# Layer 0 and layer 2 hand-over in a four-layer graph kernel: the last group's large row operations on GpSimd, layer 0's two halves together, the last two output transfers from SyncE

## Chip, cores and metric

One Trainium2 chip, one core of it. The metric is the device time of one execution in microseconds (us): three runs of the kernel before took 1114.72, 1115.99 and 1119.29 us, median 1115.99. Inside the core, TensorE (PE in the profile) does matrix products, VectorE (DVE) and ScalarE (ACT) do elementwise work, GpSimd (POOL) does elementwise work on data in SBUF only, and SyncE (SP) issues transfers. Each engine runs its own list of instructions in order.

## The reference

Four layers over 4096 nodes with 64 features and a dense 4096 x 4096 matrix `adj` of zeros and ones. Each layer is `x = layernorm(x + f(x, adj))`:

- layer 0: `h = (adj @ x + x) / deg`, then `relu([x, h] @ W + b)`, divided by its row norm
- layers 1 and 3: hyperbolic attention. For each pair i, j with an edge, a sigmoid of `left[i] + right[j]` weights the logarithmic map of x[j] at x[i]; the sums over j go through the exponential map and a projection
- layer 2: row i sums `x[j] @ weight` over its last 100 neighbours, with weights that halve from one neighbour to the next

```python
def _layernorm(x, axis=-1, eps=1e-5):
    m = jnp.mean(x, axis=axis, keepdims=True)
    v = jnp.var(x, axis=axis, keepdims=True)
    return (x - m) / jnp.sqrt(v + eps)
...
support_t = jnp.einsum('ij,ijd->id', adj_att, x_local)
return proj(expmap(x, support_t, c), c)
...
x = _layernorm(x + _L0_gnn_ref(x, adj, L0_gnn_W, L0_gnn_b), axis=-1)
```

## The kernel before

Nodes lie in four groups (`GROUPS` = 3, 2, 1, 0) of 1024, each of eight blocks (`WB`) of 128 partitions. One tile of a group's rows, `grp(...)`, is 128 x 512 floats (eight blocks of 64 features); one number for each row, `nums(...)`, is 128 x 8. Every layer walks over the four groups of target nodes and, inside each, over the 32 source blocks j from last to first, two blocks (one `g`) to a 1 MB load of `adj` from the SyncE queue into one of six buffers (`load`).

Two kinds of work share the engines. The pair work fills most of the time. In attention (`attend`, L1025) one block j needs six matrix products into `z` (L1059, L1062, L1065), a sigmoid and a square on ScalarE (L1074, L1077), one VectorE operation (L1080), and once for each g a VectorE operation over 128 x 2048 (L1082) and eight products that add up (L1037). Call the two VectorE operations T (L1080, 128 x 1024, reads PSUM and SBUF) and S (L1082, 128 x 2048, reads SBUF twice). The row work turns a finished group's sums into the next layer's tables. It is written as Python generators that `later(...)` puts into two queues; after each block of pairs `tick` lets each queue emit its next few instructions, and what a generator yields says after how many ticks it goes on. PE and ACT keep the order in which instructions were emitted in layers 0 and 2 (`manual_schedule`), a planner places the rest.

For one group that ends layer 0 (`end_0`, L1357) the row work is: for each half of the group, eight pairs of products into a PSUM tile (L1365, L1366), a reciprocal and two VectorE operations (L1369, L1371, L1373); then relu, a square on GpSimd (L1378), a row sum, an inverse root, two 128 x 512 operations (L1384, L1385); then `norm_rows` and `prepare`. `end_2` does the same after layer 2, with its own beginning (L1488, L1492, L1498).

- `norm_rows` (L862): mean, difference, square on GpSimd (L869), row sum (L872), inverse root of ten small operations, and L877, which writes the next layer's `x`.
- `prepare` (L882) and its inner `second`: small operations give `ym` (L895); L896 makes `y` from `x` and `ym`; ScalarE casts `y` three times (L899 to L901) into `ys` and `yd`; GpSimd fills ten extra columns from `hl` (L907 to L912); L915 writes the rest of `ys` (the part of `y` that the cast lost); L921 makes `w` from `x` and `g`; L923 makes `xe` from `w` and `m`, the operand of L1037. PE then turns `ys` and `yd` block by block (L943, 32 products) through PSUM, ScalarE copies each of the four results into `hi_lo`, `lo_hi`, `src` and `dst` (L947), eight products give L955, L965 reads them, and `left` and `right` follow (L975 to L977), after a logarithm on ScalarE (L950, L951).

The last group, 0, ends a layer, so its row work lies beside the first pairs of the next attention layer. `attend` calls `need((layer, 2 * g // WB))`, so the pairs of blocks 7 to 0, the last quarter of a pass, stand behind group 0's tables.

`spare` (a list) holds a second PSUM tile for row work in layers 0 and 2; `take` goes back and forth between the two tiles, and `held` counts those in use. `spare_ends` after layer 0 runs ticks until none is held.

At the end of an attention layer `move` (L1098) does the row work of a group's sums: on GpSimd for groups 3, 2 and 1, on VectorE for group 0. After layer 3 `store` (L1611) sends a group of `out` from the ScalarE queue (L1612).

Of the kernel before, what the change touches and what calls it, by code (L numbers as in the profile page):

```python
# [10 lines left out]
F32 = mybir.dt.float32  # L11
# [8 lines left out]
P = 128  # L20
N = 4096
D = 64
# [3 lines left out]
SB = W // P  # L26
# [5 lines left out]
WB = WW // P  # L32
# [26 lines left out]
def gnn_stack_kernel(  # L59
# [15 lines left out]
    nc = tc.nc  # L75
    V = nc.vector
# [492 lines left out]
    def stream(fits):  # L569

        with ExitStack() as st:
# [10 lines left out]
            GROUPS = tuple(reversed(range(NW)))  # L582
# [8 lines left out]
            queues, place, done, held = ([], []), [0, 0], set(), []  # L591
# [54 lines left out]
            def soon():  # L646


                return 0 if place[0] in (0, 2) else 1
# [7 lines left out]
            def near():  # L657

                return 3 if place[0] == 0 else 1
# [21 lines left out]
            def free():  # L681
                while held:
                    yield 1
# [18 lines left out]
            def grp(name, bufs=None):  # L702
                kw = {"bufs": bufs} if bufs else {}
                return row.tile([P, WB, D], F32, name=name, **kw)

            def nums(name, n=WB):
                return row.tile([P, n], F32, name=name)

            def over(v):
                return v[:, :, None].to_broadcast([P, v.shape[1], D])  # L710

            def rsqrt(a, name):

# [60 lines left out]
            xe = keep.tile([P, NB, D], F32, name="xe")  # L774
# [23 lines left out]
            ys = keep.tile([P, WB, 3 * D + 10], F16, name="ys")  # L798
# [43 lines left out]
            def curved(c, name, least):  # L842
# [16 lines left out]
                V.tensor_scalar(short, root, least, None, ALU.mult)  # L859
                return c, c2, sc, rsc, of_y, root, short, by_root, by_short  # L860

            def norm_rows(layer, s, v, x2_to):  # L862

                m, v2, sq = nums("n_m"), nums("n_v2"), grp("sq")
                V.tensor_reduce(m, v, AX.X, ALU.add)
                V.tensor_scalar(m, m, 1.0 / D, None, ALU.mult)
                yield soon()
                V.tensor_sub(v, v, over(m))  # L868
                nc.gpsimd.tensor_mul(sq, v, v)  # L869
                yield soon()  # L870
                yield soon()
                V.tensor_reduce(v2, sq, AX.X, ALU.add)  # L872
                yield soon()
                V.tensor_scalar(m, v2, 1.0 / D, 1e-5, ALU.mult, ALU.add)
                r = rsqrt(m, "n_r")
                yield soon()
                V.tensor_mul(x_of(layer)[:, blocks(s), :], v, over(r))  # L877
                V.tensor_mul(x2_to, r, r)
                V.tensor_mul(x2_to, x2_to, v2)
                yield soon()  # L880

            def prepare(layer, s, att, b_att, curve, least, good, small):  # L882
# [3 lines left out]
                at, cols = blocks(s), slice(s * WW, (s + 1) * WW)  # L886
                xg, bg, rbg = x_of(layer)[:, at, :], b[:, at], rb[:, at]
# [5 lines left out]

                ym, y = nums("ym"), grp("y")
                V.tensor_scalar(ym, rbg, sc, None, ALU.mult)  # L895
                V.tensor_mul(y, xg, over(ym))  # L896

                def second():
                    nc.scalar.copy(ys[:, :, :D], y)  # L899
# [11 lines left out]
                    for k, of in ((7, 0), (8, 0), (9, 1)):  # L911
                        nc.gpsimd.tensor_scalar(  # L912
                            ed[:, :, k], hl[:, :, of], -2.0 / UNIT, None, ALU.mult
                        )
                    V.tensor_sub(ys[:, :, D : 2 * D], y, ys[:, :, :D])  # L915

                    m, g, w = nums("m"), nums("g"), grp("xw")
                    V.tensor_scalar(g, cx2[:, at], 1.0, 1.0 / D, ALU.add, ALU.mult)
                    V.tensor_scalar(m, rbg, CUBE / UNIT, None, ALU.mult)
                    yield 1  # L920
                    V.tensor_add(w, xg, over(g))  # L921
                    yield 1
                    V.tensor_mul(xe[:, at, :], w, over(m))  # L923

                    q, q1, t = nums("q"), nums("q1"), nums("tt")
                    V.tensor_scalar(q, x2[:, at], least, c, ALU.max, ALU.mult)
# [27 lines left out]
                    for k in range(WB):  # L954
                        nc.tensor.matmul(  # L955
                            p[:, k, :], hi_lo[:, s * WW + k * P : s * WW + (k + 1) * P], att,
                            start=True, stop=True,
# [32 lines left out]
                    yield 1  # L990

                later(second(), True, after(small))
                yield 1

# [252 lines left out]
            def supports(s):  # L1247
# [40 lines left out]
                out=enter, in_=pass_by, compare_op=ALU.is_gt, fill=0.0, base=0,  # L1288
# [14 lines left out]
            with ExitStack() as lp:  # L1303
# [10 lines left out]
                xw = own.tile([P, NB, D], F32, name="xw")  # L1314
                sum_w = own.tile([P, D + 1], F32, name="sum_w")
                count_w = own.tile([D + 1, D + 1], F32, name="count_w")
# [39 lines left out]

                def end_0(s, tops):  # L1357
                    z = grp("z0")
                    for h, (top, low) in enumerate(tops):
                        yield from free()  # L1360
                        t = take(F32, P, SB, P)
                        for k in range(SB):
                            cols = slice(k * P, (k + 1) * P)
                            to = t[:, k, : D + 1]
                            nc.tensor.matmul(to, top[:, cols], sum_w, start=True, stop=False)  # L1365
                            nc.tensor.matmul(to, low[:, cols], count_w, start=False, stop=True)  # L1366
                        at = slice(s * WB + h * SB, s * WB + (h + 1) * SB)
                        d = nums("deg", SB)
                        V.reciprocal(d, t[:, :, D])  # L1369
                        zz = z[:, h * SB : (h + 1) * SB, :]  # L1370
                        V.tensor_mul(zz, t[:, :, :D], over(d))  # L1371
                        held.pop()
                        V.tensor_add(zz, zz, xw[:, at, :])  # L1373
                        if h == 0:
                            yield near()
                    V.tensor_scalar(z, z, 0.0, None, ALU.max)
                    sq, n2 = grp("sq"), nums("n2")
                    nc.gpsimd.tensor_mul(sq, z, z)  # L1378
                    yield 1
                    V.tensor_reduce(n2, sq, AX.X, ALU.add)  # L1380
                    V.tensor_scalar(n2, n2, 1e-24, None, ALU.max)
                    n = rsqrt(n2, "n")
                    yield 1
                    V.tensor_mul(z, z, over(n))  # L1384
                    V.tensor_add(z, z, x0[:, blocks(s), :])  # L1385
                    yield 1
                    yield from norm_rows(1, s, z, x2[:, blocks(s)])
                    yield from prepare(
                        1, s, att1, batt1_sb, curve1, 1e-15, good[:, 0], 70
                    )  # L1390

                with tc.manual_schedule(engines=FIXED):
                    for s in GROUPS:
# [3 lines left out]
                        for g in reversed(range(NB // 2)):  # L1397
# [5 lines left out]
                            for k in (1, 0):  # L1403
                                j = 2 * g + k
                                for lhs, accs, m in parts:
                                    for h in range(2):
                                        at = k * WW + h * W
                                        nc.tensor.matmul(  # L1408
                                            accs[h][:m], lhs[:, j, :], edge[:, at : at + W],
                                            start=j == BLOCKS[0], stop=j == BLOCKS[-1],  # L1410
                                        )
                            if g == s * WB // 2 + 1:

                                for lhs, accs, m in parts:
                                    for h in range(2):
                                        for k in range(SB):
# [3 lines left out]
                                                start=False, stop=False,  # L1420
# [9 lines left out]
                        tops = []  # L1430
                        for h in range(2):
                            top = sb.tile([P, W], F32, name="top")
                            nc.scalar.copy(top, sums[h])
                            low = sb.tile([D + 1, W], F32, name="low")
                            nc.scalar.copy(low, counts[h][: D + 1])
                            tops.append((top, low))
                        later(end_0(s, tops))
                        if s > 0:
                            own_of = linear(0, s - 1, w0_sb[:D, :], own_part)
# [169 lines left out]
            place[0] = 3  # L1609

            def store(s):  # L1611
                nc.scalar.dma_start(out[:, blocks(s), :], x_of(4)[:, blocks(s), :])  # L1612
                yield 1

            attention(3, curve3, (4, 1, 1, 1), store)


            V.tensor_reduce(fits, odd, AX.X, ALU.add)
            V.tensor_scalar(fits, fits, 0.0, None, ALU.is_equal)
            t, g = nums("m1", 1), nums("g1", 1)  # L1620
# [80 lines left out]
```

## Time and profile before

| what | us |
|---|---|
| median of three runs | 1115.99 |
| the profiled execution | 1117.97 |
| its span | 1116.2 |
| PE busy (share of the span) | 996.4 (89%) |
| DVE busy | 912.1 (82%) |
| ACT busy | 803.4 (72%) |
| POOL busy | 271.0 (24%) |
| layer 0, its loads | 0 to about 183 |
| first pairs of layer 1 on DVE | 201.8 |
| first pairs of layer 3 on DVE | 763.5 |
| last S of layer 3 | 1077.2 |

The page of the profile gives busy time for each engine, then the span in 40 slices, the transfers, the chain of waits that ended last, and groups of instructions. The timeline lists single instructions: start in us, duration in us, engine, line, operation, what it writes and reads, and in square brackets the idle time of the engine before it and what ended that. A busy share of 82% for DVE is an average: it is near full in the attention layers and low in layers 0 and 2 and in the last 40 us.

### The profile page before, as it was taken

The numbers are of one execution on the slowest core, as the hardware profiler recorded it, in microseconds if no ns is written. First come the engines' busy times: TensorE is split into PE (matmuls) and PEld (weight loads), VectorE is DVE, ScalarE is ACT, GpSimd is POOL, SyncE is SP. The second block draws the span as 40 slices with busy tenths as digits, with TensorE's granted clock in tenths as the row PEclk, the third lists the DMA queues.
The fourth block names the chain that finished last, engine by engine and source line by source line (L and its number), as shares of the span: only waits on it lengthen the run. The fifth ranks groups of instructions, "written<-read, shape, count | busy, mean of one in ns | idle before, by whom it ended". The sixth has DMA issues, their size and how long they took to land.

```text
span 1116.2 us, 13744 instructions
## 1 busy us (share of the span) xinstructions
PE 996.4 (89%) x4861; PEld 393.9 (35%) x4949; DVE 912.1 (82%) x1452; ACT 803.4 (72%) x892; POOL 271.0 (24%) x649
## 2 busy tenths in 40 slices
PE   4998889789999999998998997788899999999960
PEld 2455455233333333332333332223333333333320
DVE  5677977999999999999366476447989999999965
ACT  0013122989999999896776788889899999998940
POOL 0011210010144443424500010000001544345281
PEclk8899999899999999999999999899899999999995
DMA  8899999546576576663987986587456766666300
GB/s 339 346 422 376 366 423 382 204 136 243 195 238 219 184 244 217 218 210 130 360 306 275 370 277 228 203 276 252 166 194 221 247 215 216 238 224 224 126 1 23
DMA packets 38581, 271.63 MB, mean 243 GB/s; under 512 B 4710, under 2 KB 4710, under 8 KB 5734
## 3 DMA queue, kind: packets, MB, share of 16 engines
q1 hardware_dynamic: 37440, 269.50, 66.4%
q10 hardware_dynamic: 1062, 1.15, 0.3%
q8 instruction: 41, 0.67, 0.2%
q14 instruction: 38, 0.31, 0.1%
HBM read 269.58 MB, written 1.05 MB: 242 GB/s over the span
## 4 chain that ended last, share of the span: by engine, by line
PE 58%; DVE 22%; ACT 9%; POOL 4%; DMA 4%; issue 3%; ACTq 0%; SPq 0%; POOLq 0%; DVEq 0%
PE acc L1037 14%; PE z L1563 9%; DVE t L1082 8%; DVE t L1080 6%; PE z L1062 6%; PE acc L1408 6%; PE z L1059 6%; PE z L1065 6%; PE acc L1575 3%; DMA edges<-in_adj_dram 3%; ACT sq L1077 3%; ACT sq L1570 3%; ACT sig L1074 2%; PE z L1575 1%; PE aux L943 1%
## 5 line engine op out<-in xcount | busy, mean ns | idle before, releaser
L1080 DVE SCALAR_TENSOR_TENSOR t<-z,sig 128x1024 f32<-128x1024 f32 x256 | 308.9, 1218 | 13.8 <-ACT sq L1077 7.7
L1077 ACT ACTIVATE sq<-z,turn 128x1024 f32<-128x1024 f32 x256 | 278.1, 1112 | 46.2 <-PE z L1065 17.8
L1082 DVE SCALAR_TENSOR_TENSOR t<-sq,t 128x2048 f32<-128x2048 f32 x128 | 297.4, 2323 | 0.5
L1074 ACT ACTIVATE sig<-left_b,right 128x1024 f32<-128x1024 f32 x256 | 286.2, 1147 | 1.8 <-DVE t L1080 1.3
L1037 PE MATMUL acc<-t,xe 128*64 128x512 f32 x1024 | 255.6, 611 | 18.4 <-DVE t L1082 17.9
L1062 PE MATMUL z<-lo_hi,hi_lo 128*128 128x512 f16 x512 | 194.6, 380 | 3.8 <-issue 1.0
L1065 PE MATMUL z<-dst,src 74*128 74x512 f16 x512 | 195.6, 382 | 0.0
L1059 PE MATMUL z<-edges,two_i 128*128 128x512 bf16 x462 | 181.5, 393 | 8.1 <-DVE t L1080 8.1
L1570 ACT ACTIVATE sq<-z,at_edge 128x512 bf16<-128x512 f32 (+1 forms) x192 | 149.4, 829 | 44.4 <-PE z L1563 41.3
L838 DVE SCALAR_TENSOR_TENSOR t<-edges 128x2048 bf16<-128x2048 f32 x32 | 73.0, 2288 | 52.8 <-DMA edges<-in_adj_dram 52.8
L1037 PEld LDWEIGHTS acc<-t,xe 128*64 128x64 f32 x1024 | 63.8, 137 | 147.5 <-issue 83.6
L1563 PE MATMUL z<-edges,pass_by 128*128 128x512 bf16 x241 | 87.6, 400 | 18.4 <-ACT sq L1570 17.6
L1059 PEld LDWEIGHTS <-two_i 128*128 128x128 bf16 x512 | 50.2, 98 | 127.5 <-issue 82.8
L1408 PE MATMUL acc<-edges,first 128*128 128x512 bf16 x241 | 78.0, 400 | 16.1 <-DMA edges<-in_adj_dram 15.5
L1563 PE MATMUL z<-edges,enter 128*128 128x512 bf16 x240 | 85.0, 397 | 0.5
L1408 PE MATMUL acc<-edges,third 128*65 128x512 bf16 x256 | 81.4, 400 | 0.9 <-issue 0.4
L838 DVE SCALAR_TENSOR_TENSOR junk<-edges 128x2048 bf16<-128x2048 f32 x32 | 73.1, 2286 | 4.6 <-DMA edges<-in_adj_dram 4.3
L1065 PEld LDWEIGHTS <-src 74*128 74x128 f16 x512 | 49.3, 96 | 70.5 <-issue 8.4
L1062 PEld LDWEIGHTS <-hi_lo 128*128 128x128 f16 x512 | 50.4, 98 | 58.0 <-issue 12.5
L1575 PE MATMUL acc<-sq,halves 128*64 128x512 bf16 x384 | 61.6, 398 | 2.6 <-issue 1.6
L869 POOL TENSOR_TENSOR sq<-z 128x512 f32<-128x512 f32 x8 | 14.1, 1759 | 162.2 <-DVE z L868 139.5
L1133 POOL TENSOR_TENSOR w_att<-x,u 128x512 f32<-128x512 f32 x6 | 15.6, 2599 | 142.9 <-ACT u L1128 142.9
(375 smaller groups left out, 939.4 us busy)
## 6 DMA issues: line engine op xcount, KB each, us to landing
edges<-in_adj_dram SPq DMA_DIRECT2D x256, 1024.0 KB, 5.0
x<-in_x_dram SPq DMA_DIRECT2D x4, 256.0 KB
out_dram<-x ACTq DMA_DIRECT2D x4, 256.0 KB
w_sb<-in_L_gnn_W_dram ACTq DMA_DIRECT2D x1, 32.0 KB, 5.9
w_twice<-in_L_gnn_weight_dram ACTq DMA_DIRECT2D x2, 16.0 KB, 8.2
given<-in_L_gnn_b_dram ACTq DMA_DIRECT2D x1, 0.2 KB
given<-in_L_gnn_bias_dram ACTq DMA_DIRECT2D x1, 0.2 KB
given<-in_L_gnn_b_att_dram ACTq DMA_DIRECT2D x1, 0.0 KB
```

The lines of the kernel that those rows point to most:

```text
L838: V.scalar_tensor_tensor(junk, a, 0.0, a, ALU.not_equal, ALU.not_equal, accum_out=odd[:, n : n + 1])
L1037: it = nc.tensor.matmul(acc[h * D : (h + 1) * D, :], xe[:, j, :], t[:, k, h * W : (h + 1) * W], start=j == BLOCKS[0], stop=j == BLOCKS[-1],)
L1059: nc.tensor.matmul(half, two_i, edge[:, at : at + W], start=True, stop=False)
L1062: nc.tensor.matmul(half, hi_lo[:, of], lo_hi[:, to], start=False, stop=False)
L1065: last = nc.tensor.matmul(half, src[:, of], dst[:, to], start=False, stop=True)
L1074: nc.scalar.activation(sig, left_b, AF.Sigmoid, bias=right[:, j : j + 1])
L1077: nc.scalar.activation(sq[:, k], zp, AF.Square, bias=turn, scale=-1.0 / UNIT)
L1080: V.scalar_tensor_tensor(t[:, k], zp, 0.0, sig, ALU.max, ALU.mult)
L1082: V.scalar_tensor_tensor(t, sq, HIGH**2, t, ALU.add, ALU.mult)
L1408: nc.tensor.matmul(accs[h][:m], lhs[:, j, :], edge[:, at : at + W], start=j == BLOCKS[0], stop=j == BLOCKS[-1],)
L1563: nc.tensor.matmul(z[:, h : h + W], lhs, rhs[:, h : h + W], start=j == BLOCKS[0], stop=True, skip_group_check=True,)
L1570: nc.scalar.activation(w, z[:, :n], AF.Exp, bias=at_edge, scale=-LN2)
```

## The change

A helper `large_on(s)` picks GpSimd for group 0 and VectorE for the others, and five 128 x 512 operations go through it: L877, L896, L915, L921, L923. It acts after layer 0 and after layer 2, so on ten instructions in all. In `end_0` both halves take their PSUM tiles and issue their products one after the other where `spare` is there, and VectorE's part for both follows with no yield between. The transfers of groups 1 and 0 to `out` go to the SyncE queue.

```diff
+            def large_on(s):
+                return nc.gpsimd if s == GROUPS[-1] else V
...
-                V.tensor_mul(x_of(layer)[:, blocks(s), :], v, over(r))
+                large_on(s).tensor_mul(x_of(layer)[:, blocks(s), :], v, over(r))
...
-                V.tensor_mul(y, xg, over(ym))
+                large_on(s).tensor_mul(y, xg, over(ym))
...
-                    V.tensor_sub(ys[:, :, D : 2 * D], y, ys[:, :, :D])
+                    large_on(s).tensor_sub(ys[:, :, D : 2 * D], y, ys[:, :, :D])
...
-                    V.tensor_add(w, xg, over(g))
+                    large_on(s).tensor_add(w, xg, over(g))
                     yield 1
-                    V.tensor_mul(xe[:, at, :], w, over(m))
+                    large_on(s).tensor_mul(xe[:, at, :], w, over(m))
...
-                    for h, (top, low) in enumerate(tops):
-                        yield from free()
-                        t = take(F32, P, SB, P)
...
-                        held.pop()
-                        V.tensor_add(zz, zz, xw[:, at, :])
-                        if h == 0:
+                    yield from free()
+                    for some in ((0, 1),) if spare else ((0,), (1,)):
+                        ts = []
+                        for h in some:
+                            top, low = tops[h]
+                            t = take(F32, P, SB, P)
...
+                            ts.append((h, t))
+                        for h, t in ts:
...
+                            V.tensor_mul(zz, t[:, :, :D], over(d))
+                            V.tensor_add(zz, zz, xw[:, at, :])
+                        if some == (0,):
                             yield near()
+                    held.clear()
...
-                nc.scalar.dma_start(out[:, blocks(s), :], x_of(4)[:, blocks(s), :])
+                queue = nc.sync if s <= 1 else nc.scalar
+                queue.dma_start(out[:, blocks(s), :], x_of(4)[:, blocks(s), :])
```

More of the change, by code (lines that the diff above doesn't have):

```diff
@@ L1358, in end_0 @@
                     z = grp("z0")
-                    for h, (top, low) in enumerate(tops):
-                        yield from free()
-                        t = take(F32, P, SB, P)
[L1362 to L1371, printed above, removed]
-                        held.pop()
-                        V.tensor_add(zz, zz, xw[:, at, :])
-                        if h == 0:
+                    yield from free()
[4 more added lines that the diff above has]
+                            t = take(F32, P, SB, P)
+                            for k in range(SB):
+                                cols = slice(k * P, (k + 1) * P)
+                                to = t[:, k, : D + 1]
+                                nc.tensor.matmul(to, top[:, cols], sum_w, start=True, stop=False)
+                                nc.tensor.matmul(to, low[:, cols], count_w, start=False, stop=True)
+                            ts.append((h, t))
+                        for h, t in ts:
+                            at = slice(s * WB + h * SB, s * WB + (h + 1) * SB)
+                            d = nums("deg", SB)
+                            V.reciprocal(d, t[:, :, D])
+                            zz = z[:, h * SB : (h + 1) * SB, :]
+                            V.tensor_mul(zz, t[:, :, :D], over(d))
+                            V.tensor_add(zz, zz, xw[:, at, :])
+                        if some == (0,):
                             yield near()
+                    held.clear()
                     V.tensor_scalar(z, z, 0.0, None, ALU.max)
```

## The prediction

> **What bounds the kernel now.** I read the busy time by stage first. Columns: stretch in us, its length, then busy us (and instructions) of PE, PE's weight load, DVE, ACT, POOL, then PE's clock, DMA share, GB/s.
>
> ```profile
> 182.00:202.00 20.00, 12.99 (x86) 8.34 (x85) 10.84 (x27) 9.25 (x11) 1.04 (x1) 0.84 0.88 364
> 202.00:262.00 60.00, 53.38 (x255) 20.39 (x259) 57.54 (x107) 53.67 (x56) 5.74 (x8) 0.94 0.51 173
> 763.00:830.00 67.00, 60.81 (x278) 23.12 (x281) 63.02 (x105) 58.09 (x61) 3.22 (x8) 0.95 0.54 194
> 1072.00:1092.50 20.50, 7.39 (x26) 1.84 (x22) 7.52 (x8) 2.06 (x3) 16.44 (x51) 0.77 0.00 1
> ```
>
> Four places hold the edits. Where group 0's rows lie beside pairs (202 to 262, 763 to 830) DVE is full to 96% and 94%; at 182 to 202 and 1072 to 1092 no engine but POOL is full, so something waits. The wait list of the end and the chain of waits name it:
>
> ```profile
> ACT ys L1128 <- POOL x L1218: 8.9, 1, 8.9
> ```
>
> ```profile
> 1090.91 1.19 POOL x L1218
> 1092.12 0.34 ACTq L1612
> 1092.50 0.39 ACT ys L1128
> ```
>
> ACT's list holds group 1's output transfer (L1612) ahead of the copy that begins group 0's last row work (L1128). The transfer waits for GpSimd's `x` of group 1 until 1092.1; the copy's products were over at 1083.68 + 0.71 = 1084.39. So 8.1 us of the end are a transfer standing in a queue. The handover from layer 0 reads alike in ACT's timeline:
>
> ```profile
> 192.31 1.01 ACT L947 COPY lo_hi<-aux 128x1024 f16<-128x1024 f16 x1 [4.24 <-PE aux L943]
> 196.69 1.28 ACT L1074 ACT_TABLE_LOAD   x1 [3.37 <-DVE z L1373]
> ```
>
> The first sigmoid of layer 1 (its memory was layer 0's) stands behind L1373 of group 0's second half, 196.53. The first half had been done at 190.1; the second half's products ran at 193.5 to 195.4. The last view is how DVE and GpSimd get on:
>
> ```profile
> 367.15 1.04 POOL L1214 TENSOR_TENSOR w_att<-x,p 128x512 f32<-128x512 f32 x1
> 368.15 1.04 POOL L1215 TENSOR_TENSOR u<-u,q 128x512 f32<-128x512 f32 x1
> 369.27 3.11 POOL L1218 TENSOR_TENSOR x<-u,w_att 128x512 f32<-128x512 f32 x1
> ```
>
> ```profile
> 365.76 2.57 DVE L1080 SCALAR_TENSOR_TENSOR t<-z,sig 128x1024 f32<-128x1024 f32 x2
> 368.24 3.09 DVE L1082 SCALAR_TENSOR_TENSOR t<-sq,t 128x2048 f32<-128x2048 f32 x1
> ```
>
> GpSimd runs at its own 1.04 us beside T (L1080, one input from PSUM). Against S (L1082, both inputs from SBUF) whoever comes second waits: S took 3.09 where it takes 2.28 alone, then the next GpSimd operation took 3.11.
>
> **What the Trainium skill says.** "GPSIMD Engine Reference", section Specifications: GpSimd's SBUF interfaces are shared with VectorE, with contention when a DVE instruction has two SBUF inputs. The trace agrees (3.09 against 2.28). The same page, section Performance versus the Vector engine, gives 4497 against 2293 ns for an add of 2048 elements, ratio 1.96; here 128 x 512 takes 1.04 against 0.68 us, ratio 1.5, and I use these. "DMA: Bandwidth & Descriptors", section Issuing engines are not separate DMA queues: another issuing engine saves only its sequencer's time. That holds for the transfer; the gain here is what the issuing engine had waiting behind it, which the trace shows as 8.9 us.
>
> **The change part by part.** The built order of instructions of both kernels shows what moves.
>
> *Transfers.* Group 1's transfer leaves ACT's list; nothing else now stands between `sums` (L1088) and the copies. The copy starts at about 1084.45 in place of 1092.50: 8.05 us. SP's list has then: the last load, group 1's transfer, the read of `n_fit`, group 0's transfer, the branch. The loads end long before; the read stands behind group 1's `x` (about 1093) and is over well before group 0's `x`. Issue costs the same (0.34 us), and ACT loses a read that came after its last transfer; I count 0 (bounds -0.5 and +0.5). What is late next: group 0's chain on DVE now runs beside GpSimd's end of group 1. DVE's row chain would start at 86.65 (1094.67 less 8.05), GpSimd has three 128 x 512 operations at 1088.8 to 1092.1 (1.04 + 1.05 + 1.18 = 3.3 us). Small two-input operations on DVE are in no row of before seen waiting, so the loss lies between 0 and 3.3; I take 1.3. GpSimd's own delay costs nothing, its transfer has 12 us to spare. Part: -8.05 + 1.3 = -6.75.
>
> *Halves together.* In groups 3 to 1 the products only move within layer 0, whose end is set by loads (the last lands at 182.7) and PE; 0 (bounds -1, +1). For group 0: PE's new order turns group 1's `hi_lo` before the last layer-0 products and `lo_hi` right after them, then nine of the sixteen pairs, six `z`, seven more. ACT copies `top` and `low` from 184.7 (four at 0.5: to 186.6) and `lo_hi` to 187.6, which frees the second PSUM tile. First half 185.7 to 187.5 (eight pairs took 2.1 us), `z` to 190.2 (six at 0.43, the low clock), rest to 191.8. DVE's reciprocal and two operations (1.05 us) end L1373 at about 193.0 in place of 196.5. Sigmoid and the serial chain on DVE up to the first T (201.76) move with it: -3.5. If PE's `z` block the second half no less than before, -1; if all sixteen pairs run at once, -4.5.
>
> *Five operations on GpSimd after layer 0.* DVE loses five at 0.60 us (start to start): 3.0 us less. GpSimd gets five at 1.04. Its new order is `x`, `w`, `y`, the eight small fills from `hl`, `xe`, and the rest of `ys` (L915) last. Count from the last step of the inverse root, L722, about 227.1 on the clock of before. S follows it at once on DVE and holds the ports for 2.2, so `x` ends at 3.25. `g` comes at 5.05, `w` ends at 6.2, as does the wait of the next S; `ym` is there at 5.75. Whichever of `y` and S goes first, `y` ends at 7.3 or 9.5. The fills (about 0.15 each) lie around the next S (10 to 12.2), `xe` takes to about 14.3, L915 to 15.4, that is 242.5 where it ended at 234.9 before. PE stands at L943 for L915, ACT behind PE with squares 15 and 16. From L915 the trace of before takes 9.9 us to L965, with copies and products by turns; on the new order I get 4.7 to the square that S number 8 needs and 9.3 to L965. DVE has 14.7 us of pairs and small operations to run until S 8, then waits to 20.1, S to 22.3, L965 at 24.7, the logarithm at 27.8, the next S ends at 30.2. Before, the same S ended at 254.9 = 27.8, with the same T done. So +2.4, of which I keep +2.0, since a first start without S saves some. Bounds: -3.0 (all of DVE's saving, no wait) and +5 (each of `y` and L915 held by one more S).
>
> *After layer 2.* Here T, not S, follows the last L722 (790.7), so `x` runs at once; `w` 795.9 to 796.9, `y` to 798.0, fills, one S, `xe`, L915 to about 804.0 against 801.0. But PE turned `ys` only at 801.75 before, since it had stood 2.35 us for the T behind DVE's row operations (799.25), and that T now comes at 796.9. Turning starts 2.3 us later, L965 comes at about 815 against 813.2, and by then one more S is done (before: 815.9). I take +0.5 (bounds -3, +5).
>
> *Sum.* -6.75 - 3.5 + 2.0 + 0.5 = -7.75. The durations are those of the profiled execution (1117.97 us, span 1116.2, 1.8 around it), 2.0 above the median. The edits lie at the ends and seams of stages and don't scale with that, so I take the sum from the median: 1115.99 - 7.75 = 1108.2.
>
> **The rivals.**
>
> - *GpSimd's part hides.* If L915 comes in time, both seams gain (-1 and -2 against +2.5 of mine), and the end loses nothing to ports (-1.3): 1108.2 - 3 - 2.5 - 1.3 = 1101.4. For it: T leaves the ports free. Against: each of these ten operations meets S, which runs for 2.28 us of every 4.6.
> - *The ports give it back.* The end loses 3.3 in place of 1.3, the seams 4.5 and 3.5 in place of 2.0 and 0.5: 1108.2 + 2.0 + 2.5 + 3.0 = 1115.7, no difference. For it: the 3.11 above.
> - *Slower: L915 last in GpSimd's order.* Place: PE at L943, with `z` behind it and ACT and DVE behind `z`. Price: one S, 2.2 us, for each GpSimd operation that comes second. The other edits gain 10.25; the kernel is slower once the two seams together lose more than that, about five us each, and by 0.5% from 15.8. All ten held by an S are 22 us, of which DVE's saved 6 come off: +16 gives 1115.99 - 10.25 + 16 = 1121.7. Against: three of the five have T or small operations next to them in the new order.
> - *The transfer's move gains nothing,* were ACT to stand at that point for another reason: 1108.2 + 6.75 = 1115. The wait list shows one wait only there, and the products before it ended at 1084.39.
>
> **How the numbers follow.** My forecast (1105 to 1111.5) has 0.50, GpSimd hidden 0.15, the ports 0.25, slower 0.06, the transfer 0.04. A measurement of this kernel tells about 0.5% from no change, that is below 1110.4 or above 1121.6. Faster takes most of the forecast (0.45) and the first rival: 0.60. Same: the rest of the forecast, the ports and the transfer, 0.34. Slower 0.06. The range goes from the first rival's centre to just above the second's: 1102 to 1116, leaving out about 0.07 below and 0.12 above.
>
> **What would show it.** In the new profile: the first L1128 to `ys` follows its products at once, and GpSimd's `x` of group 1 ends beside DVE's small operations, longer than 0.17 us if ports matter (then the -6.75 is too large). L1373 of group 0's second half about 10.3 us after the last load of layer 0 landed at 182.7 (before: 13.9), that is 193.0, with the first T 3.5 us earlier. L915 on GpSimd about 7.7 us later than before against its S in layer 1, 3 us in layer 3; a DVE wait for ACT's square or L955 of 5 us or more in layer 1. The forecast is wrong if the seam of layer 1 gains over 4 us or if either seam loses over 5.

## The result and the profile after

The changed kernel takes 1115.47 us (median of 20 runs, 1110.26 to 1122.42) against 1113.74 for the kernel before beside it (20 runs); the ratio is 1.0018, 95% interval [1.0002, 1.0035]. I had forecast 1108.2. The measured time lies inside my range of 1102 to 1116 only because that range reached up to no change; I had forecast 7.75 us less, and the kernel takes 2.0 more (0.2 to 3.9). The profiled execution took 1110.26 us with a span of 1108.3, that of the kernel before 1117.97 and 1116.2. These two executions differ by layer 0 before any edit acts: the end of the first group lies at 50.25 us against 56.57, a matter of how fast the loads came. So I compare from marks inside the program. From the first T of layer 1 to the 16th S, kernels that share these instructions agree to 0.3 us (84.9, 85.1 and 85.2 us in three of them); later stages agree to 1 to 3 us, for a reason given below the table of experiments. From the first T to the last VectorE instruction the kernel before needs 909.8 us, the changed kernel 912.8.

Three of the four stages that the prediction read, in the trace of after (same columns; the windows lie against the first T and the last S as they did before):

```profile
170.48:190.48 20.00, 15.15 (x112) 9.81 (x111) 14.43 (x40) 9.57 (x13) 1.04 (x1) 0.98 0.97 395
190.48:250.48 60.00, 49.84 (x226) 18.66 (x226) 52.16 (x91) 45.30 (x48) 11.47 (x13) 0.86 0.41 151
1070.73:1091.23 20.50, 6.84 (x31) 2.23 (x27) 14.59 (x29) 3.45 (x6) 16.86 (x51) 0.83 0.01 2
```

At the end of the program DVE now works 14.59 of 20.5 us, not 7.52: the end was pulled together. In the 60 us behind the first T, DVE fell from 57.5 to 52.2, ACT from 53.7 to 45.3, PE's clock from 0.94 to 0.86, and PE handled 226 instructions, not 255. Five operations left DVE there, but none left PE or ACT: these two stood. The wait list of that seam (188 to 256 us):

```profile
PE aux L948 <- POOL ys L920: 6.9, 1, 6.9
...
DVE lr L970 <- PE aux L960: 4.0, 1, 4.0
...
ACT ys L904 <- POOL y L901: 2.0, 1, 2.0
...
DVE m L967 <- POOL xe L928: 1.9, 1, 1.9
```

L920 is the rest of `ys` (L915 before), L948 the first turn, L970 the read of the eight products (L965 before). Before, PE stood 1.5 us at that place, for DVE (202 to 262 us):

```profile
PE aux L943 <- DVE ys L915: 1.5, 1, 1.5
```

The chain of waits through the same place:

```profile
226.00 0.25 POOL ys L912
226.25 2.20 POOL ys L913
...
228.72 0.59 POOL yd L917 x3
229.30 0.98 POOL xe L928
230.28 1.08 POOL ys L920
...
231.41 1.04 PE aux L948 x8
232.45 1.90 PE acc L1042 x2
234.34 0.97 PE aux L948 x8
235.31 3.00 PE acc L1042 x6
```

From 226.0 to 231.4 the kernel's longest chain runs through GpSimd, which before was on no path here: a fill of 128 x 16 numbers takes 2.20 since S holds the ports, then `xe`, which PE doesn't need yet, and then L920. GpSimd's and DVE's timelines show both sides of the sharing:

```profile
217.47 3.02 POOL L882 TENSOR_TENSOR x<-z,n_r 128x512 f32<-128x512 f32 x1 [17.73 <-DVE n_r L722]
...
226.16 2.29 POOL L913 COPY ys<-hl 128x16 f16<-128x16 f16 x1
```

```profile
219.52 1.01 DVE L883 TENSOR_TENSOR x<-n_r 128x8 f32<-128x8 f32 x1
...
223.47 1.02 DVE L965 TENSOR_SCALAR q<-q 128x8 f32<-128x8 f32 x1
...
225.07 1.00 DVE L989 TENSOR_TENSOR g<-rb 128x8 f32<-128x8 f32 x1
...
230.32 1.07 DVE L967 TENSOR_SCALAR m<-b,k_of_y 128x8 f32<-128x8 f32 x1 [1.88 <-POOL xe L928]
```

Each of these DVE instructions takes 0.15 to 0.23 where no GpSimd operation lies beside it. Each starts while GpSimd works on 128 x 512 and ends with it: four times about 0.85 us. DVE gave away five operations of 0.60 (3.0 us) and got back 3.4 us of waiting behind ports, and 1.9 for `m`.

The end of the program, ACT's and SyncE's timelines, and DVE's rows over 0.9 us beside GpSimd's last `x`:

```profile
1081.62 0.38 ACT L1133 COPY ys<-aux 128x260 f32<-128x260 f32 x1 [0.80 <-PE aux L1131]
```

```profile
1091.26 12.11 SPq L1625 DMA_DIRECT2D out_dram<-x  x2
```

```profile
1088.06 0.92 DVE L759 TENSOR_TENSOR rs_t<-r_t 128x8 f32<-128x8 f32 x1
1089.02 0.97 DVE L739 SCALAR_TENSOR_TENSOR rs_t<-rs_t,t 128x8 f32<-128x8 f32 x1
1090.22 1.03 DVE L759 TENSOR_TENSOR rs_t<-r_t 128x8 f32<-128x8 f32 x1
```

The copy of group 0's sums follows its products at once (0.80 of waiting, before 8.9), and the same price shows on DVE: three small operations at about 0.97. The last S to the last DVE instruction is 27.08 us, before 34.37.

### The profile page after: what moved, and what is told of

It reads as the page before. It is cut to its first block, busy times and chain, and to the rows that moved or that the text cites. A ratio compares the mean times of both kernels' runs of the same rounds, so it can differ in the third digit from the quotient of the medians.

```text
span 1108.3 us, 13825 instructions
## 1 busy us (share of the span) xinstructions
PE 1003.5 (91%) x4949; PEld 392.3 (35%) x4949; DVE 918.5 (83%) x1442; ACT 803.9 (73%) x892; POOL 279.5 (25%) x659
## 3 DMA queue, kind: packets, MB, share of 16 engines
HBM read 269.58 MB, written 1.05 MB: 244 GB/s over the span
## 4 chain that ended last, share of the span: by engine, by line
PE 54%; DVE 26%; ACT 8%; DMA 5%; POOL 4%; issue 3%; ACTq 0%; SPq 0%; POOLq 0%; DVEq 0%
PE acc L1042 14%; PE z L1574 9%; DVE t L1087 9%; DVE t L1085 8%; PE z L1064 6%; PE z L1067 6%; PE z L1070 6%; DMA edges<-in_adj_dram 4%; PE acc L1586 4%; PE acc L1419 3%; ACT sq L1082 3%; ACT sq L1581 2%; DVE junk L838 2%; PE z L1586 1%; ACT sig L1079 1%
## 5 line engine op out<-in xcount | busy, mean ns | idle before, releaser
L1085 DVE SCALAR_TENSOR_TENSOR t<-z,sig 128x1024 f32<-128x1024 f32 x256 | 308.8, 1217 | 16.2 <-ACT sq L1082 10.3
L1082 ACT ACTIVATE sq<-z,turn 128x1024 f32<-128x1024 f32 x256 | 277.8, 1111 | 44.2 <-PE z L1070 18.2
L1064 PE MATMUL z<-edges,two_i 128*128 128x512 bf16 x512 | 201.4, 393 | 7.4 <-DVE t L1085 7.3
L1070 PE MATMUL z<-dst,src 74*128 74x512 f16 x512 | 195.6, 382 | 0.0
L1419 PE MATMUL acc<-edges,first 128*128 128x512 bf16 x256 | 80.5, 396 | 15.4 <-DMA edges<-in_adj_dram 15.2
L1574 PE MATMUL z<-edges,enter 128*128 128x512 bf16 x256 | 90.5, 396 | 0.0
L1067 PEld LDWEIGHTS <-hi_lo 128*128 128x128 f16 x512 | 50.4, 98 | 57.5 <-issue 12.1
```

What stands on the lines that cost most here:

```text
L1064: nc.tensor.matmul(half, two_i, edge[:, at : at + W], start=True, stop=False)
L1067: nc.tensor.matmul(half, hi_lo[:, of], lo_hi[:, to], start=False, stop=False)
L1070: last = nc.tensor.matmul(half, src[:, of], dst[:, to], start=False, stop=True)
L1082: nc.scalar.activation(sq[:, k], zp, AF.Square, bias=turn, scale=-1.0 / UNIT)
L1085: V.scalar_tensor_tensor(t[:, k], zp, 0.0, sig, ALU.max, ALU.mult)
L1419: nc.tensor.matmul(accs[h][:m], lhs[:, j, :], edge[:, at : at + W], start=j == BLOCKS[0], stop=j == BLOCKS[-1],)
```

## Experiments

Every kernel below is built from the kernel before or from the changed one. The table has what was measured and four stages of each trace. T is L1080 and S L1082 of the kernel before; S16 is the 16th S of layer 1, which has 64, S128 the last S of layer 3, "end" the last VectorE instruction. "Stand" is PE's longest idle time within 20 us of the last L722 of the seam of layer 1. Times in us.

| kernel | ratio to before, 95% | first T to S16 | S16 to S64 | S64 to S128 | S128 to end | stand |
|---|---|---|---|---|---|---|
| before | | 85.1 | 236.0 | 554.4 | 34.4 | 1.5 |
| after | 1.0018 [1.0002, 1.0035] | 93.5 | 236.0 | 556.2 | 27.1 | 6.9 |
| e1_store | 0.9949 [0.9928, 0.9971] | 84.9 | 235.9 | 554.3 | 28.3 | 1.5 |
| e2_halves | 1.0003 [0.9979, 1.0027] | 87.9 | 236.0 | 554.1 | 34.3 | 2.0 |
| e3_five | 1.0075 [1.0045, 1.0105] | 90.2 | 236.7 | 556.2 | 34.3 | 6.3 |
| e4_no_five | 0.9947 [0.9930, 0.9964] | 88.4 | 236.8 | 553.8 | 27.0 | 2.0 |
| e5_ysub | 1.0051 [1.0032, 1.0070] | 88.6 | 236.0 | 555.6 | 34.3 | 5.1 |
| e6_w_xe | 1.0064 [1.0034, 1.0094] | 89.2 | 235.9 | 559.3 | 34.3 | 4.8 |
| e7_four | 1.0034 [1.0016, 1.0052] | 86.7 | 236.7 | 554.7 | 34.3 | 3.3 |
| e8_own_m | 1.0091 [1.0059, 1.0124] | 89.8 | 236.0 | 558.6 | 34.3 | 6.4 |
| e9_five_late | 1.0032 [1.0013, 1.0051] | 85.8 | 235.9 | 558.6 | 34.3 | 2.0 |
| e10_none_late | 0.9937 [0.9916, 0.9959] | 85.5 | 236.5 | 555.0 | 28.2 | 1.6 |
| e11_all_late | 1.0017 [1.0000, 1.0034] | 92.8 | 236.0 | 556.2 | 27.1 | 2.9 |
| e12_idle_two | 1.0035 [1.0021, 1.0048] | 87.2 | 235.9 | 555.9 | 34.3 | 2.3 |
| e13_store_late | 0.9932 [0.9906, 0.9959] | 83.8 | 235.8 | 554.2 | 27.1 | 1.3 |
| e14_all_spread | 0.9979 [0.9956, 1.0002] | 89.8 | 236.2 | 557.8 | 27.0 | 4.5 |
| e15_none_spread | 0.9917 [0.9890, 0.9945] | 85.4 | 236.9 | 555.2 | 28.3 | 1.6 |
| e16_layer3 | 1.0022 [1.0004, 1.0040] | 85.2 | 235.9 | 555.7 | 34.3 | 1.5 |

Single stages behind S16 must not be read too finely. In all 18 traces S48 to S64 takes 80.8 us where PE's granted clock stays at 1.00, and 81.5 in the five (e3, e4, e7, e10, e15) where it falls to 0.50 for 3.4 us. From S64 to the first T of layer 3, where no edit acts, it is 240.7 to 240.8 us with 17.1 us at half clock, 241.4 to 241.6 with 20.5, 242.7 to 243.8 with 23.9 and 243.9 with 27.3. So differences of 0.7 in the fourth column and of up to 3 in the fifth go with the clock.

Which theory I held changed on the way. Theory A, from the trace of after: the five operations lose at the seam of layer 1 because L920 comes last on GpSimd and PE stands for it. Rival B: each GpSimd operation costs by itself, by holding small DVE operations. Rival C (first four kernels): the halves cost at the seam. From the ninth kernel on, "Theory C" is another thing, A widened: whatever makes the turn late, engines then stand in order.

### One part of the change at a time

e1_store, e2_halves and e3_five are the kernel before with one part of the diff each, whose core is, in this order,

```
-                nc.scalar.dma_start(out[:, blocks(s), :], x_of(4)[:, blocks(s), :])
+                queue = nc.sync if s <= 1 else nc.scalar
+                queue.dma_start(out[:, blocks(s), :], x_of(4)[:, blocks(s), :])
```

```
-                    for h, (top, low) in enumerate(tops):
+                    for some in ((0, 1),) if spare else ((0,), (1,)):
```

```
-                V.tensor_mul(x_of(layer)[:, blocks(s), :], v, over(r))
+                large_on(s).tensor_mul(x_of(layer)[:, blocks(s), :], v, over(r))
```

(and the same for the other four operations). e4_no_five is the changed kernel with

```
-                return nc.gpsimd if s == GROUPS[-1] else V
+                return V
```

e1_store:

> The kernel before with one part of the change alone: the output transfers of groups 1 and 0 are issued by SyncE. Theory A (the transfer gives its gain, the five operations on GpSimd lose it at the seam of layer 1): 7 us faster than the kernel before, ratio 0.9937, with the first ys copy of group 0 1.4 us after its sums. Rival C (the transfer only shifts a wait): within 2 us of before. My prediction had 8.05 us for this part without GpSimd's operations beside DVE.

Measured: -5.7 us (interval -8.0 to -3.2), by the trace -6.1 from S128 to the end, the first `ys` copy 1.39 us after the copy of its sums began, and 0.04 after its products ended. As Theory A says.

e2_halves:

> The kernel before with the two halves of a group's sums of layer 0 taken together, alone. Theory A: 2.4 us faster (ratio 0.998), all of it between the last top copy of layer 0 and the first T. Rival C (the regrouped row work displaces other work and costs inside layer 0 or at the seam what it gains): no gain, or slower by 1 us or more. My prediction had 3.5 us for it.

Measured: +0.3 us (-2.3 to +3.0), and +2.8 from the first T to S16. Rival C is right in this: what is gained ahead of the first T is lost behind it.

e3_five:

> The kernel before with the five large row operations of the last group of layers 0 and 2 on GpSimd, alone. Theory A: slower by 8.9 us (ratio 1.008): 8.5 at the seam of layer 1, 0.4 at that of layer 3. Rival C (the loss at the seam belongs to the halves): slower by no more than 3 us. My prediction had 2.5 us slower.

Measured: +8.4 us (+5.0 to +11.7): 5.1 up to S16, 0.7 in the rest of layer 1 (the clock's; e4_no_five has it too), 1.8 from S64 to S128. The size is A's, but the seam of layer 1 has 5.1 of it, not the 8.5 that I had read off the trace of after; the difference is the halves'.

e4_no_five:

> The changed kernel with the five operations back on VectorE: transfers and halves alone. Theory A: 9 to 10 us faster than the kernel before (ratio 0.991 to 0.992), that is faster than both. Rival C (halves cost at the seam): 7 us at most, the transfer's part.

Measured: -5.9 us (-7.8 to -4.0): the transfer's part alone, as Rival C had it. The three parts add up to -5.7 + 0.3 + 8.4 = +3.0, and the change measured +2.0.

### Which of the five

e5_ysub, e6_w_xe and e7_four move only the operations named, for example e5_ysub from the kernel before:

```
-                    V.tensor_sub(ys[:, :, D : 2 * D], y, ys[:, :, :D])
+                    large_on(s).tensor_sub(ys[:, :, D : 2 * D], y, ys[:, :, :D])
```

e8_own_m keeps all five on GpSimd and adds a tile:

```
-                    V.tensor_scalar(m, bg, of_y, None, ALU.mult)
+                    m2 = nums("m2")
+                    V.tensor_scalar(m2, bg, of_y, None, ALU.mult)
```

with `m2` in place of `m` in the two later uses.

e5_ysub:

> The kernel before with one of the five operations on GpSimd: the rest of ys (the subtraction that PE's first turn waits for). Theory A (this operation, last in GpSimd's order with the eight small fills ahead of it, holds PE and with it ACT and DVE): at least 3 us slower (ratio 1.003 or more), with PE standing 4 us or more for it in layer 1. Rival B (each GpSimd operation costs by itself, through small DVE operations held beside it): 1.7 us, a fifth of the five's 8.4.

Measured: +5.7 us (+3.6 to +7.8), PE stands 5.1. One operation does two thirds of the harm of five, and its own 1.11 us is the least of it: GpSimd's timeline has the fills ahead of it (seven of them, not eight).

```profile
234.14 2.52 POOL L912 COPY ys<-hl 128x16 f16<-128x16 f16 x1
...
237.09 1.11 POOL L920 TENSOR_TENSOR ys<-y,ys 128x512 f16<-128x512 f32 x1
```

e6_w_xe:

> The kernel before with w and xe on GpSimd, x, y and ys on VectorE. Theory A: nothing that PE turns waits for these two, so between 1 us faster and 1 us slower. Rival B: two fifths of 8.4, 3.4 us slower or more, as small DVE operations (and the one that rewrites m, which xe reads) stand behind GpSimd.

Measured: +7.1 us (+3.8 to +10.5), where A expected at most 1. A is wrong in this form. The DVE timeline shows how these two reach the turn after all:

```profile
226.66 1.04 DVE L716 TENSOR_SCALAR rt<-q 128x8 int32<-128x8 int32 x1
...
230.36 0.29 DVE L967 TENSOR_SCALAR m<-b,k_of_y 128x8 f32<-128x8 f32 x1 [1.34 <-POOL xe L928]
...
230.75 2.28 DVE L1087 SCALAR_TENSOR_TENSOR t<-sq,t 128x2048 f32<-128x2048 f32 x1
232.96 0.68 DVE L920 TENSOR_TENSOR ys<-y,ys 128x512 f16<-128x512 f32 x1
```

DVE waits for `xe` to have read `m`, then comes an S that the new order has ahead of L920, and only then the rest of `ys`; it ends 12.8 us after the last L722, 8.9 before. PE stands 4.75 us for that S and turns late.

e7_four:

> The kernel before with x, y, w and xe on GpSimd and the rest of ys on VectorE. Theory A: a wait of 3 us or less for y is left of the 6.3 us that PE stood, so at most 3 us slower than before. Rival B: four fifths of 8.4, about 6.7 us slower.

Measured: +3.8 us (+1.8 to +5.8): between the two. L920, back on DVE, ends 10.8 us after L722.

e8_own_m:

> The kernel before with all five on GpSimd, and a tile of its own for the second value of m, so that DVE doesn't wait for xe to have read the first. Theory A: still 7 us slower or more than before, since DVE has PE's stand to wait for in any case. Rival B: 2 to 4 us of the 8.4 come back (1.9 of waiting at each of the two seams).

Measured: +10.1 us (+6.6 to +13.8). Taking DVE's wait for `xe` away gives nothing back; PE still stands 6.4.

So in the seam of layer 1 the loss goes with PE's stand at a late turn, by whatever way the turn came late. PE's stand over the 1.5 of before, and the loss up to S16, go together in these five kernels (e7, e5, e6, e3, e8): 1.8 and 1.6, 3.6 and 3.5, 3.3 and 4.1, 4.8 and 5.1, 4.9 and 4.8; and in after against e4_no_five: 4.9 and 5.1.

### Taking the stand away, and the ports alone

In e9_five_late (from e3_five), e10_none_late (from e4_no_five) and e11_all_late (from after) the last group's steps from the first turn on are emitted later:

```
-                    yield 2 * near()
+                    yield (32 if s == GROUPS[-1] else 2 * near())
```

In layer 3 the traces have the turns where they were. In layer 1 the edit does more than move the turns, since DVE's order is planned anew: the rest of `ys` ends 12.1 us after L722 in e10_none_late (8.9 in e4_no_five), 17.1 in e11_all_late (14.0 in after), 14.3 in e9_five_late (13.2 in e3_five).

e12_idle_two adds to the kernel before, behind DVE's `w` and `xe`, for the last group only:

```
+                        dum = grp("sq")
+                        nc.gpsimd.tensor_add(dum, xg, over(rbg))
...
+                        nc.gpsimd.tensor_mul(dum, xg, over(rbg))
```

e9_five_late:

> The kernel before with all five operations on GpSimd (as in e3_five) and the turns of the last group emitted later: in layer 1 PE's list has about 33 halves of pairs ahead of the first turn where it had 30; layer 3 is as in e3_five. Theory C (what the five cost at the seam of layer 1 is PE standing for a late ys, while pairs that are ready lie behind the turn in its list): PE no longer stands more than 2 us there, and of the 5.1 us that e3_five lost from the first T to S number 16 at least 3.5 come back; about 4 us slower than before in all (ratio 1.003 to 1.005), layer 3's part. Rival B (small DVE operations held beside GpSimd, wherever PE turns): as e3_five, ratio 1.007.

Measured: +3.6 us (+1.4 to +5.7), as Theory C says. With the five still on GpSimd PE stands 2.03 us, not 6.3, and first T to S16 falls from 90.2 to 85.8, 0.8 above before. PE's timeline:

```profile
239.73 1.03 PE L948 MATMUL aux<-ident,ys 128*128 128x128 f16 x8 [2.03 <-POOL ys L920]
```

e10_none_late:

> The changed kernel with the five operations on VectorE (as e4_no_five) and the last group's turns emitted later in layer 1. Theory C: PE's stand of 2.0 us at the turn goes, 1 to 3 us faster than e4_no_five, so a ratio to the kernel before of 0.992 to 0.994. Rival B: as e4_no_five, 0.9947.

Measured: -7.0 us (-9.4 to -4.6), 2.9 us less than e4_no_five up to S16.

e11_all_late:

> The changed kernel, all five on GpSimd, with the last group's turns emitted later in layer 1. Theory C: the 6.9 us stand of PE at the turn goes with most of what it cost, so 4 to 6 us faster than the changed kernel, ratio to the kernel before 0.996 to 0.998. Rival B: as the changed kernel, 1.002.

Measured: +1.9 us (0.0 to +3.8). A miss: PE's stand fell to 2.9, yet 0.7 us came back up to S16. The wait list of this kernel (205 to 285 us) says who stands instead:

```profile
DVE t L1085 <- ACT sq L1082: 7.1, 6, 4.9
...
POOL y L901 <- DVE m L924: 3.7, 1, 3.7
ACT hi_lo L952 <- PE aux L948: 3.7, 1, 3.7
...
PE aux L948 <- POOL ys L920: 2.9, 1, 2.9
...
ACT lo_hi L952 <- PE aux L948: 2.5, 1, 2.5
```

L920 ends 17.1 us after L722 here (14.0 in after), as GpSimd waits 3.7 for DVE ahead of `y` (0.5 in after); ACT holds its copies of the turns ahead of the squares, and DVE waits for the squares. Against e10_none_late the five cost 7.3 us up to S16. So in the changed kernel PE's stand alone is not shown to be the cost.

e12_idle_two:

> The kernel before with two more 128x512 two-input operations on GpSimd after layers 0 and 2, at the places in GpSimd's order that w and xe have in e6_w_xe; their results are used by nothing, and VectorE still computes w and xe. It tells the cost of sharing ports alone. Rival B: 2 x 0.9 us at each seam, about 3.6 us slower. Theory C (e6_w_xe lost 7 us through the chain from w and xe to the turn): within 1.5 us of the kernel before.

Measured: +3.9 us (+2.3 to +5.3). Here Rival B has the number and C not: two operations that nothing waits for cost as much as B's arithmetic. In layer 1 DVE's order is that of before up to S16, so the price can be read off single lines (DVE, then GpSimd):

```profile
228.40 1.02 DVE L903 TENSOR_SCALAR hl<-rb 128x8 f16<-128x8 f32 x1
```

```profile
228.36 1.04 POOL L925 TENSOR_TENSOR sq<-x,rb 128x512 f32<-128x512 f32 x1 [22.18 <-DVE q L966]
...
231.53 1.04 POOL L929 TENSOR_TENSOR sq<-x,rb 128x512 f32<-128x512 f32 x1
```

L903 takes 0.86 us more than the 0.16 of such an instruction, the DVE instruction beside the second one (the second value of `m`) 0.82 more, S number 6 comes 1.7 later and S16 2.1 (PE's stand grew by 0.9 with it). So B is no rival but a second term: 0.85 us for each GpSimd operation that meets small DVE operations, more than the 0.60 that a move takes off DVE.

### What was still open

e13_store_late is e1_store with the `yield` line above. e14_all_spread and e15_none_spread are e11_all_late and e10_none_late with 44 in place of 32. e16_layer3 is e3_five with

```
-                return nc.gpsimd if s == GROUPS[-1] else V
+                return nc.gpsimd if s == GROUPS[-1] and layer == 3 else V
```

e13_store_late:

> Transfers from SyncE alone (as e1_store) and the last group's turns emitted later in layer 1; no halves, nothing moved to GpSimd. If the halves gain 2 to 4 us once the turns don't hide it, this kernel is 2 to 4 us slower than e10_none_late (ratio to the kernel before about 0.996 to 0.997). If the halves gain nothing, it equals e10_none_late, 0.993 to 0.994.

Measured: -7.6 us (-10.5 to -4.6), no slower than e10_none_late: the halves gain nothing that can be measured. This kernel is also what e9_five_late is without the five (the transfers act only at the end). With late turns the five then cost 2.0 us up to S16 (85.8 against 83.8). So without the halves some 3 of the 5.1 go with the place of the turns. For the 2.0 that are left, DVE's held instructions (3.4 us, and up to 1.9 more before `m`) less the 3.0 that it saved come to between 0.4 and 2.3.

e14_all_spread:

> The changed kernel with the last group's steps from the first turn on emitted later still in layer 1: the first turn stands where it stood in e11_all_late, the other three lie apart among the pairs. Theory C (engines standing in order at the turns and at their copies): from the first T to S number 16 at least 3 us less than e11_all_late's 92.9, and a ratio to the kernel before of 0.996 to 0.999. Rival (only the lateness of the first turn counts): as e11_all_late, 1.0017.

Measured: -2.3 us (-4.9 to +0.2); first T to S16 3.0 less than e11_all_late, though PE's one stand grew to 4.5. So it isn't the first turn's stand alone: the later turns and ACT's copies of them, close together, had held the pairs.

e15_none_spread:

> As e10_none_late (transfers and halves, five operations on VectorE), with the other three turns spread further. Theory C: as e10_none_late within 1.5 us, as PE stands only 1.6 us there; ratio 0.992 to 0.995. If spreading delays left and right of the last group past the pairs that need them, 2 us slower or more.

Measured: -9.3 us (-12.3 to -6.1), S16 as in e10_none_late. e10, e13 and e15 can't be told apart by their times, nor from e1_store: the intervals overlap. All four beat both kernels, and e1_store does so with the least change.

e16_layer3:

> The kernel before with the five operations on GpSimd after layer 2 alone. From e3_five's trace (1.9 us lost in layer 3): 2 us slower, ratio 1.001 to 1.003. If the loss there is as large as in the traces of e8_own_m and e9_five_late (4.2 us), ratio 1.004. My prediction had 0.5 us for it.

Measured: +2.5 us (+0.4 to +4.5), by the trace 1.3 from S64 to S128.

## Why the prediction was wrong, step by step

*Transfers, -6.75: right.* Alone -5.7 (-8.0 to -3.2), by the traces -6.1 alone and -7.3 in the changed kernel. The copy came 8.07 us nearer to its products (8.05 forecast). The loss beside GpSimd, taken as 1.3 between 0 and 3.3, is 2.3 from that copy to the end. The stage is 1.2 us shorter in five kernels with the transfer on SyncE (after, e4, e11, e13, e14) than in three others (e1, e10, e15). That is the clock: the last eight products of L1037 take 1.94 us at 1.00 in the five and 3.42 to 3.45 at 0.54 in the three. So 1.2 of the 7.3 in the changed kernel is nothing that I had worked out.

*Halves, -3.5: right up to the point where I stopped reading, wrong as a gain.* I followed them to the first T. That comes 2.8 us earlier on average (mean of seven traces with the halves together 195.6, of eleven without 198.4, standard error 1.3). The mark that I had named is sharper: L1373 of the second half ends 9.5 us after the last load of layer 0 landed (10.3 forecast, 13.9 before), and 9.5 to 12.3 in the seven against 13.0 to 18.5 in the eleven. But from the first T to S16 they cost 2.8 (e2_halves over before) and 3.5 (e4_no_five over e1_store). The first part of it can be seen in the DVE timeline of e4_no_five:

```profile
200.88 1.23 DVE L1085 SCALAR_TENSOR_TENSOR t<-z,sig 128x1024 f32<-128x1024 f32 x1 [0.68 <-ACT sq L1082]
...
202.85 1.05 DVE L980 TENSOR_TENSOR left<-lr,f 128x8 f32<-128x8 f32 x1
```

The row work of group 1 keeps its own time, so it lies later against the first T; a T waits 0.68 for its square, and `left` now meets GpSimd's `sq` (1.04 us from 202.85) and takes 1.05, where in e1_store a T lay beside it. That is 1.6 us at S number 2. With later turns 1.7 are left at S16 (e10_none_late 85.5, e13_store_late 83.8), so the rest goes with the turns; by what way isn't shown.

*Five operations after layer 0, +2.0 (bounds -3 and +5): the term that failed.* Isolated, it is +5.1 (e3_five over before, and after over e4_no_five), at the upper bound. My working ended at S number 9 with +2.4; e3_five has +3.6 there, and the next S adds 1.5. Three steps can be checked in the trace of after. "L915 to 15.4": it ended 14.0 us after L722 (8.9 before), so this was slightly too late, and GpSimd waiting for S was there (`x` 3.02, a fill 2.29). "From L915 ... 9.3 to L965": 13.7, and 14.0 in e3_five. This step failed. I gave the turns and copies behind a late `ys` no more than the 9.9 us of before, but PE came back from its stand at half clock, and the pairs' `z` lay behind the turns in its list. DVE, for which I had 5.4 us of waiting up to S number 8, waited 1.0 there and then 4.0 more for L965. Third, I charged nothing to small DVE operations in the seams, although I had bounded that very price at the end of the program: 4 x 0.85 us, more than DVE's saved 3.0; the two idle operations of e12_idle_two alone cost 2.1 up to S16. DVE's 1.9 us before it rewrites `m` I had not seen either, but e8_own_m shows that it costs nothing beside the stand.

*After layer 2, +0.5: right sign, too small.* +2.5 (+0.4 to +4.5) measured, 1.3 by the trace. PE's stand doesn't grow there (2.5 against 2.4), but four small DVE operations are held as in layer 1 (1.01 to 1.07 us each, from 793.5 to 799.4 in after). From the first T of layer 3 to the last S the six kernels with all five and an unchanged `m` (after, e3, e9, e11, e14, e16) take 314.7 to 314.9 us, before 313.6, so about 1.2; e1, e10 and e15 have 313.6 too, with the clock at half for as long. The larger losses of e8 and e9 from S64 to S128 lie ahead of this seam, with the clock; e6 loses 3.0 behind the first T, and why is not shown.

*The sum.* -6.75 - 3.5 + 2.0 + 0.5 = -7.75; measured in the same order -5.7 + 0.3, and +8.4 for the five together: +3.0. So the five are off by 5.9 (8.4 against 2.5), the halves by 3.8, the transfers by 1.1, each known to about 3 us to either side. Two terms made the sign wrong: the turns behind a late `ys`, and a gain of the halves that I followed only to the first T. The rival "the ports give it back" had the total (1115.7) with the halves counted as gain; "slower" had the right place, PE at L943, but needed ten us and more. The forecast's own test, wrong "if either seam loses over 5", has just fired with 5.1.

## What to carry to other kernels

Moving an elementwise operation off a full VectorE can cost more than it saves, by what it then sits beside on GpSimd: here 0.60 us saved cost 0.85 wherever a small VectorE instruction was held. Before moving one, list what lies ahead of it in the new engine's order and what lies behind its reader: the larger part of the cost was not the operation's 1.1 us but TensorE standing 5 us longer in its in-order list. In e9_five_late, with about three more halves of pairs ahead of the turn, it worked on until 12.3 us after L722 instead of 6.9 in e3_five. And follow an edit to the next full stage, not to the next mark: the halves' 2.8 us ahead of layer 1 were gone ten S later.

## What the runs showed of the hardware

- A small VectorE instruction (128 x 8) beside a 128 x 512 GpSimd operation takes 1.00 to 1.07 us in the seams, not 0.16, whether it has one input (L965 of the changed kernel, L903 of e12_idle_two) or two (L883): it ends when the GpSimd operation ends. In the kernel before no small instruction starts beside one. The Trainium skill, "GPSIMD Engine Reference", section Specifications, names DVE instructions with two SBUF inputs or in a 2-port mode as those that contend; that L965, with one input, is held fits the second kind, but no run shows its mode. T, with one input from PSUM, ran at 1.21 to 1.23 us in these seams.
- The reverse is dearer: a fill of 128 x 16 on GpSimd takes 2.29 to 2.52 us beside S, not 0.22.
- During PE's stand the granted clock fell, and it came back late (columns as above):

```profile
231.40:235.30 3.90, 3.89 (x20) 1.89 (x21) 3.90 (x9) 2.03 (x2) 0.00 (x0) 0.50 0.00 0
235.30:238.30 3.00, 3.00 (x8) 0.76 (x8) 1.97 (x3) 2.03 (x2) 0.00 (x0) 0.62 0.03 5
238.30:246.00 7.70, 7.70 (x50) 3.27 (x50) 3.70 (x9) 5.73 (x6) 0.00 (x0) 1.00 0.08 17
```

In windows of half a microsecond the clock goes from 1.00 to 0.50 at 227.0 to 227.5, 2.8 us after PE's last product, and back at 237.5, some 6 us after the first turn. So a stand costs more than its length: eight turns took 1.04 us instead of 0.62. The Trainium skill, "TensorE: Matmul & The Clock Gate", section on the HAM clock gate, says that the array drops to half its rate after at least one idle window of about 3.4 us and needs at least one such window of sustained work to come back. The trace of after roughly agrees. The one of before doesn't: there the clock was 0.50 from 237 to 240, behind stands of only 1.5 and 1.1 us, PE having been busy for 0.85 of the 3.41 us before the fall. So in this trace two short stands close together did what a long one does.
